# Two graph layers on one core: a new order of the written-out steps, with map, messages and the output product ahead of the four cosines

## The chip, the core and the metric

The kernel runs on one core of a Trainium2 chip. The metric is device time in microseconds (us) from start to end of one execution. The engines of the core are TensorE (PE in the profile; its weight loads are PEld), VectorE (DVE), ScalarE (ACT), GpSimd (POOL) and SyncE (SP, which issues nearly all DMAs). Each works through its own queue in order and waits where an instruction needs what another engine has not finished.

## What is computed

There are 64 graphs of 256 nodes with 512 features, each with an adjacency mask. Two layers follow one another. Cut to what matters:

```python
h = relu(layernorm(x))                      # layer 0, 8 heads of 64
m = h @ map_w.T + map_b
cos_adj = (cosine(m, m) > 0.1) & mask       # per head
p = softmax(where(mask, q(m) @ k(m).T / 8, NEG)) * keep
adj = cos_adj * p
x = x + relu((adj @ (h @ gcn_map_w.T + b)) @ gcn_W.T / (adj.sum(-1) + 1))
h = relu(layernorm(x))                      # layer 1, 4 heads of 64
x = x + softmax(where(mask, q @ k.T / 8, -inf)) @ v @ Wo + bo
```

All products are in float32.

## The kernel before

The graphs are taken one after the other, in a software pipeline over five of them. In round i the kernel works on graph i (its attention and cosines of layer 0), on i+1 (its map, messages, queries and keys), on i+2 (its first layernorm and the transposing of it), on i-1 (layer 1 up to its values) and on i-2 (the output product of layer 1 and the store). The work of a round is cut into 240 small steps with names of two to four letters (`steps_of`, L697 on). The list `ORDER` (L679) gives the order in which they are written out for rounds 2 to 61. `HEAD` and `TAIL` (L1010 on) give it for the opening, with rounds 0 and 1, and for the closing, with rounds 62, 63 and what follows. The whole runs under `tc.manual_schedule()`: the order of the list is the order of each engine's queue. Nothing is moved at run time.

Steps that matter here, with their lines:

- `sc0` to `sc3`: scores of graph i for two heads each, two PSUM banks a step (L475). `ex` takes their exponential (ACT, L482), `mk` multiplies by the mask (DVE, L491), `hv` adds the two halves (POOL, L495).
- `co0` to `co3`: cosines, likewise two banks a step (L512). `un` makes the unit vectors first (DVE, L460). `up` and `fo` read the cosines from PSUM (ACT L521; DVE L528, four instructions a step). `ft` transposes by DMA (SP, L533), `fb` applies that (DVE, L543), `fa` and `fz` add up (POOL, L538).
- Seven products: the matrices are multiplied in halves with seven block products instead of eight (class `Seven`, L303). The steps of one are `X1 Xa X2 Xd X3 Xb X4 Xc X5 Xe X6 Xf X7 Xg`. `1` to `7` are products on PE (L318, L323). `1`, `3`, `4` fill bank u, `2`, `5`, `6`, `7` fill bank z and go on adding to it. `a`, `b`, `c` copy parts of u away, `d`, `e`, `f` add such a copy to z and store a quarter of the result, `g` stores the last. So `5` needs `d`, `6` needs `e`, `7` needs `f`; bank u is free after `c`, bank z after `g`. X is `m` for the map, `s` for the messages, `q` and `k` for queries and keys, `j` and `v` for layer 1's queries with keys and values, `w` for layer 1's output. The adds are DVE's (L350, with L335 and L339 for the copies of `w` and `s`); the copies and the last store of `m`, `q`, `k` are ACT's (L343), those of `j` and `v` ACT's too (L337).
- Left factors on POOL (L295 to L301): `lw` for w, `lm` for q and k, `lb` for j and v, `lh` for m and s. Product `3` needs the first, `5` the second, `6` the third, `4` the fourth.
- `av0`, `av1`: values of layer 0 (L502). `hs` (ACT), `ht` (DMA), `hj` (ACT, L572) turn them. `rt`, `rc`, `rk`, `ho`, `ha` divide and add them to x. `nb`, `pb`, `xb`, `fl`, `tr`, `jb` are the layernorm of layer 1 and its transposing by DMA; `na`, `pa`, `xa`, `pl`, `ta`, `ja` are the same for graph i+2 in layer 0.
- `sd`, `ey`, `my`, `hy`, `ay`, `zb`, `iy`, `sy`, `dv`: attention of layer 1. `sq`, `pn`, `ln`, `ls`, `li`, `sp`: the lengths for the unit vectors. `bo` adds the bias (POOL). `mt` and `ed` prepare the mask.

All PSUM tiles come from one ring of eight banks (`ring`, `bufs=8`). A tile takes the bank that has been free longest in the order of the steps, and waits for the last reader of the tile before it.

Of the kernel before, what the change touches and what calls it, by code (L numbers as in the profile page):

```python
# [158 lines left out]
def fast_path(ctx, tc, a, w, chk, out):  # L159
# [850 lines left out]
    HEAD = """  # L1010
        o.w0 o.na00 o.na01 o.nr0 o.dn0 o.xn00 o.xn01 o.tp00 o.gb o.fm0 o.fm1 o.tq00 o.tp01 o.tq01 o.ed0 o.lh00
        o.lh01 o.lh03 o.bp o.m1 o.fp1 o.lj o.ma o.fm2 o.m2 o.md o.m3 o.fm3 o.fq0 o.fq1 o.q2 o.lo
        o.m5 o.mb o.fo1 o.lh02 o.m4 o.fp2 o.mc o.fq2 o.me o.fp0 o.fo0 o.m6 o.fq3 o.fk0 o.mf o.sq1
        o.fp3 o.bo o.m7 o.mg o.fo3 o.k1 o.k2 o.fk1 o.lm0 o.fk2 o.fk3 0.na o.lm1 0.pa o.lm3 o.lm2
        o.na10 o.q1 o.na11 o.fo2 o.sq0 o.q3 o.k3 o.pn o.qa o.qb o.kb o.qd o.ln o.fs0 o.fs1 o.s1
        o.nr1 o.ka 0.xa0 0.pl00 o.q4 o.qc o.kd o.sa o.fs2 o.q5 o.k4 o.k5 o.s2 o.dn1 o.fs3 o.qe
        o.ex o.lv o.kc o.ke o.xn10 o.xn11 o.ls o.sd o.k6 o.q6 o.kf o.mt0 o.qf o.s3 0.sc2 0.ex2
        0.sc3 o.s5 o.tp10 o.fw0 o.fv0 o.fw1 o.sb o.s4 o.fj0 o.fj1 o.tp11 o.k7 0.mk2 o.li o.sc o.se
        0.hv2 o.s6 o.q7 0.xa1 0.pl10 0.ex3 o.fw2 o.kg o.qg o.tq10 o.tq11 o.sf o.s7 0.sc0 0.sc1 0.mk3
        o.sp o.ed1 0.mt o.fv1 0.un 0.hv3 o.lh10 o.sg 0.ex0 0.co2 0.fo2 0.ex1 0.co1 0.co0 0.co3 0.up2  # L1020
        0.up0 0.ft0 0.m1 0.m3 0.mk1 o.lh12 0.up3 0.ma o.fj2 0.mk0 0.up1 0.fo3 o.lh11 o.lh13 0.hv1 0.s1
        0.s3 0.m2 0.sa 0.mb 0.s2 o.lb o.l3 0.ft2 0.ta00 0.md 0.sb 0.sd 0.m4 0.m5 0.fo1 0.fa3
        0.hv0 0.fa2 0.fa1 0.ed 0.s4 0.ft3 0.mc 0.me 0.m6 0.mf 0.s5 0.m7 0.q1 0.sc 0.fo0 0.k1
        0.se 0.pl01 0.ta01 0.fb3 0.ka 0.sq1 0.qa 0.pl11 0.mg o.fv2 o.fv3 0.ft1 0.k2 0.ta10 0.fb1 0.s6
        0.q2 0.sf 0.s7 0.fa0 0.fz1 0.fz3 0.lm0 0.ta11 0.lm1 0.sq0 0.fb2 0.fb0 0.av0 1.na 0.lm3 0.av1
        0.fz0 0.hs01 0.ja0 0.ja1 0.pn 0.hs00 0.ln 0.kd o.fj3 0.q3 0.qd 0.k3 0.k5 0.kb 0.ht01 0.hs10
        0.hs11 1.m1 0.qb 0.k4 0.ls 0.ht00 0.ht10 0.ht11 0.kc 0.lh0 0.q4 0.qc 0.fz2 0.sm 0.hj00 0.ke
        0.q5 0.to 0.lm2 0.lh2 0.li 0.qe 0.k6 0.q6 0.rt 1.s1 1.s2 1.ma 0.kf 0.qf 0.lh1 1.pa
        0.lh3 0.rc 0.sg 1.rk 0.hj01 0.sp 0.hj10 0.hj11 1.m3 0.k7 0.kg 0.q7 0.qg 1.s3 1.sc2 1.sc1
        1.m2 1.mb 1.ho0 1.ho1 1.ha0 1.ha1 1.nb 1.sa 1.pb 1.ex2 1.xb0 1.sb 1.ex1 1.mk2 1.sd 1.xb1  # L1030
        1.s4 1.m4 1.s5 1.mc 1.un 1.sc0 1.ex0 1.fl00 1.sc3 1.fl01 1.fl10 1.sc 1.se 1.md 1.tr00 1.ex3
        1.co1 1.mk1 1.co0 1.s6 1.tr01 1.fl11 1.mk0 1.tr10 1.up1 1.up0 1.xa0 1.tr11 1.jb0 1.mt 1.sf 1.m5
        1.hv1 1.fo1 1.s7 1.hv0 1.fa1 1.co2 1.jb1 1.hv2 1.sg 1.xa1 1.me 1.fo0 1.fo2 1.fa0 1.lb0 1.lb1
        1.up2 1.ft0 1.pl01 1.ta01 1.co3 1.k2 1.m6 1.j1 1.ja 1.j2 1.mf 1.k1 1.up3 1.pl00 1.mk3 1.hv3
        1.pl10 1.fo3 1.j3 1.v1 1.v3 1.jd 1.m7 1.jb 1.mg 1.lb3 1.j4 1.vb 1.v2 1.v4 1.vc 1.fa2
        1.fa3 1.lb2 1.fb0 1.ka 1.ft1 1.ft2 1.ta00 1.ft3 1.fb2 1.j5 1.fb1 1.kd 1.va 1.jc 1.je 1.lm0
        1.vd 1.fb3 1.av0 1.av1 1.j6 1.q1 1.hs11 1.v5 1.hs00 1.pl11 1.jf 1.ta10 1.ja0 1.fz2 1.fz0 1.j7
        1.ve 1.v6 1.hs01 1.lm1 1.hs10 1.fz3 1.bo1 1.k3 1.jg 1.sd1 1.sd0 1.kb 1.ey1 1.ey0 1.vf 1.my1
        1.q3 1.ta11 1.ht10 1.v7 1.lm3 1.k4 1.sq1 1.qb 1.k5 1.q4 1.kc 1.sq0 1.pn 1.my0 1.ln 1.ke
        1.q2 1.bo0 1.vg 1.ht11 1.ja1 1.ht00 1.hy1 1.hy0 1.fz1 1.lh0 1.ls 1.lm2 1.lh1 1.ht01 1.zb 1.iy  # L1040
        1.sy 1.qa 1.qd o.fw3 1.hj00 1.lh3 1.li 1.sp 1.sm 1.ay 1.to 1.ed 1.lh2 1.q5 1.rt 1.k6
        1.qc 1.qe 1.oy 1.q6 1.hj01 1.kf 1.rc 1.qf 1.k7 1.rq 1.hj10 1.hj11 1.q7 1.qg 1.kg 1.zq
    """.split()
    TAIL = """
        2.rk 2.m1 2.ma 2.sc0 2.ex0 2.sc1 2.sc2 2.ex1 2.ho0 2.ho1 2.ha0 2.dv 2.sc3 2.s1 2.s3 2.w2
        2.s2 2.ex3 2.ha1 2.nb 2.mk3 2.lw0 2.m2 2.pb 2.xb0 2.un 2.sa 2.m3 2.xb1 2.ex2 2.w1 2.lw1
        2.fl00 2.mb 2.sd 2.md 2.sb 2.wa 2.wd 2.mk2 2.fl11 2.s5 2.fl01 2.m4 2.mc 2.mk0 2.m5 2.fl10
        2.s4 2.lw3 2.hv0 2.co0 2.sc 2.me 2.se 2.co2 2.up2 2.up0 2.m6 2.s6 2.w3 2.mk1 2.mf 2.m7
        2.wb 2.fo0 2.mt 2.tr00 2.tr01 2.tr10 2.tr11 2.w4 2.jb0 2.hv2 2.wc 2.hv3 2.w5 2.mg 2.co3 2.lw2
        2.hv1 2.we 2.ft0 2.jb1 2.lb0 2.lb1 2.lm0 2.fo2 2.fo3 2.co1 2.fo1 2.j1 2.lb2 2.lb3 2.fa1 2.rr  # L1050
        2.w6 2.fa0 2.fa3 2.fa2 2.v1 2.up3 2.v3 2.up1 2.lm1 2.j3 2.ja 2.ft2 2.j2 2.wf 2.va 2.w7
        2.v2 2.jd 2.vd 2.jb 2.j4 2.sf 2.v5 2.jc 2.j5 2.q1 2.vb 2.v4 2.ft3 2.je 2.qa 2.vc
        2.wg 2.ft1 2.ve 2.j6 2.k1 2.ka 2.v6 2.jf 2.fb0 2.fz0 2.j7 2.fb1 2.fz1 2.vf 2.lm3 2.v7
        2.sq1 2.jg 2.vg 2.sq0 2.av0 2.fb3 2.hs00 2.hs01 2.pn 2.fz3 2.sd0 2.ey0 2.ht00 2.fb2 2.sd1 2.av1
        2.k2 2.q3 2.ln 2.rq 2.my0 2.ey1 2.fz2 2.hy0 2.my1 2.hy1 2.q2 2.sm 2.zb 2.hj00 2.hs10 2.hs11
        2.ls 2.ht01 2.ht10 2.ht11 2.qb 2.to 2.hj01 2.q4 2.qc 2.rt 2.qd 2.iy 2.kd 2.rc 2.q5 2.hj10
        2.qe 2.hj11 2.k3 2.kb 1.rk 2.lm2 2.q6 2.ay 1.ho0 2.k4 2.kc 2.st 2.k5 2.oy 1.ho1 1.ha0
        1.ha1 2.qf 1.nb 2.li 1.pb 2.ke 2.q7 2.k6 2.kf 2.s7 2.qg 1.xb0 1.fl00 1.xb1 2.k7 2.kg
        2.zq 1.sc0 2.sp 1.un 1.fl01 1.sc1 1.sc2 2.sg 1.fl10 1.sc3 1.ex0 1.co0 1.ex1 2.sy 1.ex2 1.mk0
        1.mk1 1.co2 1.fl11 1.tr00 1.tr01 1.tr10 1.ex3 1.co1 1.rq 1.up0 1.up1 1.up2 1.jb0 1.mk2 c.se0 c.se1  # L1060
        1.mk3 c.se2 c.se3 1.dv 1.fo2 1.lw0 1.co3 1.fo0 1.tr11 1.ft1 1.w1 1.lw1 1.lw3 1.jb1 1.up3 1.w3
        1.fo1 2.bo0 1.rr 1.wa 2.bo1 1.lb0 1.lb1 1.lb3 1.lw2 1.w2 1.wd 1.j2 1.lb2 1.j1 1.w5 1.ja
        1.wb 1.w4 1.ft2 1.ft0 1.ft3 1.fb2 1.fb1 1.v1 1.wc 1.fb0 1.fo3 1.fb3 1.j3 1.av0 1.av1 c.sm0
        c.sm1 1.bo1 c.sm3 c.vs1 c.vs0 1.jb 1.va c.fi c.sm2 1.we 1.w6 c.to c.hb1 1.rt c.hb0 1.wf
        1.rc c.rk 1.w7 1.j4 1.jd 1.j5 1.jc c.hm0 c.hm1 1.je 1.v2 1.vd 1.v3 1.vb 1.j6 1.v4
        1.vc c.hp0 c.nb0 c.hp1 1.jf 1.v5 1.bo0 1.j7 c.nb1 1.jg 1.ve 1.v6 c.nr c.dn c.xn0 c.xn1
        1.vf 1.sd0 1.sd1 1.v7 c.tp0 c.tp1 1.ey0 1.my0 1.ey1 c.rq 1.vg c.tq0 1.my1 1.ay c.tq1 1.hy0
        1.hy1 0.lb0 0.lb1 0.j1 0.ja 1.zb 0.v1 0.lb3 0.j3 1.zq 0.jb 1.iy 0.lb2 0.j2 1.sy 0.j4
        0.jd 0.jc 0.j5 0.v3 0.vb 0.v2 0.je 0.j6 0.va 0.v4 1.oy 0.vd 0.v5 0.jf 0.vc 0.j7
        0.jg 0.ve 0.v6 0.sd0 0.sd1 0.vf 0.v7 0.ey0 0.ey1 0.dv 0.lw0 0.w2 1.wg 0.my0 0.my1 1.st  # L1070
        0.w1 0.lw1 0.w3 0.wa 0.wd 0.wb 0.vg c.zl c.zi0 0.lw3 0.ay c.zm0 0.bo0 0.w5 0.w4 c.zi1
# [336 lines left out]
```

## Time and profile before

| | |
|---|---|
| median of 3 runs | 3538.68 us (3538.03 to 3538.77) |
| the profiled execution | 3538.69 us |
| its span, first to last instruction | 3536.9 us |
| mean granted TensorE clock | 0.999 |
| matmuls | 29365 |
| DMA | 258.30 MB, mean 73 GB/s |
| one round in the middle | 54.67 us |

In a timeline line the columns are start in us, length in us, engine, line of the kernel, operation, what is written and read, shapes (stationary tile, moving tile), and the number of instructions that are merged into the line. In square brackets stands the idle time before it and what ended it. Matmuls overlap, so the length of such a line is a little more than the time to the next start; the starts give the pace. A PE share of 100% only says that some matmul was always under way. A matmul that started late, or ended late, hides a wait in it. Lines of groups end in busy time, mean length in ns, and idle time before the group with what ended most of it. In the list of waits come total us, times and the longest.

### The profile page before, as it was taken

To read this page: it belongs to the slowest core of one execution; us is meant where nothing else is said; L and a number is where in the kernel's file an instruction comes from. 1 tells how busy PE (TensorE), PEld (TensorE's weight loads), DVE (VectorE), ACT (ScalarE), POOL (GpSimd) and SP (SyncE) were. 2 spreads that over 40 slices of the span, in tenths; PEclk is the share of its full clock that TensorE was granted. 3 is DMA by queue.
4 is the path that set the end of the run, shared out by engine and by line. 5 is a ranking of instruction groups with operands and counts; after the bars stand their busy time and mean duration, and the time that the engine had idled before them with its cause. 6 is when DMAs were issued, how large, how long until landed. Compare 5 with 4: busy or idle time off the path is not lost.

```text
span 3536.9 us, 78933 instructions
## 1 busy us (share of the span) xinstructions
PE 3521.0 (100%) x29365; PEld 3090.5 (87%) x29365; DVE 2407.6 (68%) x5037; ACT 2261.2 (64%) x5302; POOL 2693.9 (76%) x2866
## 2 busy tenths in 40 slices
...
DMA packets 650589, 258.30 MB, mean 73 GB/s; under 512 B 561980, under 2 KB 616792, under 8 KB 650200
## 3 DMA queue, kind: packets, MB, share of 16 engines
q1 hardware_dynamic: 649464, 252.62, 32.5%
...
## 4 chain that ended last, share of the span: by engine, by line
PE 98%; DVE 0%; issue 0%; ACT 0%; ACTq 0%; DVEq 0%
PE av L502 10%; PE p_q_z L323 7%; PE p_m_z L323 7%; PE p_s_z L318 7%; PE sc L475 7%; PE p_qk_z L323 6%; PE p_k_z L323 6%; PE co L512 6%; PE p_qk_u L323 5%; PE p_q_u L323 5%; PE p_k_u L323 5%; PE p_m_u L323 5%; PE p_s_u L318 5%; PE sd L475 3%; PE p_o_z L318 3%; PE p_v_z L318 3%
## 5 line engine op out<-in xcount | busy, mean ns | idle before, releaser
L495 POOL TENSOR_TENSOR d<-e 128x512 f32<-128x512 f32 x378 | 532.5, 1422 | 316.2 <-DVE e L491 165.3
L538 POOL TENSOR_TENSOR d<-d,e 128x512 f32<-128x512 f32 x504 | 633.4, 1273 | 68.4 <-DVE e L543 65.2
L489 DVE SCALAR_TENSOR_TENSOR e<-mask,e 128x1024 f32<-128x1024 bf16 x128 | 214.4, 1677 | 245.4 <-ACT e L482 245.3
L260 POOL COPY flat<-xn 128x512 uint16<-128x512 uint16 x252 | 310.7, 1261 | 58.4 <-ACT xn L252 57.5
L491 DVE TENSOR_TENSOR e<-e,mask 128x1024 f32<-128x1024 f32 x256 | 328.4, 1324 | 4.3 <-ACT e L482 2.8
L528 DVE SCALAR_TENSOR_TENSOR e<-co,e 128x256 f32<-128x256 f32 (+1 forms) x1024 | 293.9, 349 | 52.6 <-ACT up L521 33.1
L482 ACT ACTIVATE e<-sc 128x512 f32<-128x512 f32 x512 | 270.8, 601 | 75.3 <-PE sc L475 75.2
L521 ACT ACTIVATE up<-co,below 128x128 bf16<-128x128 f32 x512 | 166.8, 371 | 195.7 <-PE co L512 121.4
L252 ACT ACTIVATE xn<-xs,shift,rs 128x512 f32<-128x512 f32 x250 | 196.9, 811 | 74.8 <-POOL shift L242 74.8
L475 PE MATMUL sc<-qT,kT 64*128 64x256 f32 x2048 | 239.0, 383 | 0.0
L502 PE MATMUL av<-e,sem 128*64 128x256 f32 x2048 | 235.5, 382 | 0.0
L512 PEld LDWEIGHTS co<-nT 64*128 64x128 f32 x2048 | 185.0, 186 | 53.9 <-issue 34.6
L512 PE MATMUL co<-nT 64*128 64x128 f32 (+1 forms) x2048 | 228.9, 338 | 0.5 <-DVE nT L460 0.5
L475 PEld LDWEIGHTS sc<-qT,kT 64*128 64x128 f32 x2048 | 192.0, 186 | 29.3 <-DVE wo L83 0.3
L502 PEld LDWEIGHTS av<-e,sem 128*64 128x64 f32 x2048 | 141.2, 137 | 85.7 <-issue 20.2
L295 POOL TENSOR_TENSOR own<-own 128x128 f32<-128x128 f32 x63 | 52.0, 825 | 181.0 <-DVE own L674 181.0
L572 ACT COPY sem<-heads 128x512 uint16<-128x512 uint16 x252 | 187.0, 780 | 1.6 <-DMA heads<-avs 1.6
L443 POOL TENSOR_TENSOR lengths<-lengths,root 128x16 f32<-128x16 f32 x64 | 185.8, 2903 | 1.6 <-DMA lengths<-rn 1.6
L482 ACT ACTIVATE e<-sd 128x512 f32<-128x512 f32 x256 | 138.7, 599 | 66.4 <-PE sd L475 66.4
L205 DVE BATCH_NORM_STATS2 st<-xs 128x6 f32<-128x512 f32 x256 | 172.6, 674 | 5.8 <-DMA xs<-in_x_dram 3.6
L276 ACT COPY h1T<-turn 128x1024 uint16<-128x1024 uint16 x126 | 169.7, 1348 | 7.2 <-DMA turn<-flat 7.1
L272 ACT COPY hT<-turn 128x1024 uint16<-128x1024 uint16 x124 | 171.2, 1382 | 0.0
...
## 6 DMA issues: line engine op xcount, KB each, us to landing
...
nT<-by_rn SPq DMA_DIRECT2D x128, 256.0 KB
...
far<-up SPq DMA_TRANSPOSE x256
heads<-avs SPq DMA_TRANSPOSE x252
```

Source lines behind the costliest of these rows:

```text
L260: copy(getattr(g, what)[:, t, k, :], g.xn[t].bitcast(U16).rearrange("p (d k) -> p k d", k=2)[:, k, :])
L318: nc.tensor.matmul(region, src[:, c, :], self.wt[:, block, c, :], start=p not in self.opened, stop=True, skip_group_check=True)
L323: nc.tensor.matmul(region[:, f, :], self.wt[:, block, c, f * P:(f + 1) * P], src[:, c, :], start=p not in self.opened, stop=True, skip_gro ...
L475: nc.tensor.matmul(ps[s][:, j, :], rows[h, c, j * P:(j + 1) * P], cols[h, c, :], start=True, stop=True)
L482: nc.scalar.activation(e[:, s, :], p.rearrange("p j q -> p (j q)"), AF.Exp, scale=SCALE)
L489: nc.vector.scalar_tensor_tensor(e, m, 0.5, e, op0=ALU.is_lt, op1=ALU.mult)
L491: nc.vector.tensor_mul(e, e, m)
L495: nc.gpsimd.tensor_add(d, e[:, :, :S], e[:, :, S:])
L502: nc.tensor.matmul(av[s * DH:(s + 1) * DH, n, :], vs[:, j, (h0 + s) * DH:(h0 + s + 1) * DH], q[:, s, j * S:(j + 1) * S], start=(j == 0), s ...
L512: nc.tensor.matmul(ps[s][:, j, j * P:], g.nT[h, c, j * P:(j + 1) * P], g.nT[h, c, j * P:], start=(j == 0), stop=True, skip_group_check=True)
L528: nc.vector.scalar_tensor_tensor(e, p.rearrange("p j q -> p (j q)")[:, lo:hi], THRESHOLD, e, op0=ALU.is_gt, op1=ALU.mult)
L538: nc.gpsimd.tensor_add(g.d[c][:, :, q], g.d[c][:, :, q], g.e[c][:, :, lo:hi])
```

## The change

The three lists are written in a new order. Each holds the same steps as before (240, 512 and 451), so no instruction is added, removed or altered; the queues of the engines and the choice of banks change with the order. In `ORDER` the old list starts with the four scores and spreads map, messages and output product from before the cosines to after them (`m6`, `s6`, `m7`, `s7` come after `co1`). The new one starts with `s1 s3 m1 m3`, and has all products of `s`, `m` and `w` ahead of `co0`; queries and values follow the cosines.

```diff
     ORDER = """
-        rk sc2 ho1 ho0 sc1 sc3 ha0 dv ha1 ex2 sc0 ex3 lw0 lw1 nb w2
-        w1 w3 s1 m1 s3 wa wd wb lw3 w4 mk3 mk2 ex1 mt w5 lw2
-        s2 m3 wc we sa sd pb w6 xb0 xb1 ma fl01 s5 wf w7 m2
-        un fl00 tr00 hv3 fl10 fl11 wg md sb mb m4 tr01 ex0 st m5 tr10
-        mk1 mk0 hv1 mc s4 sc co3 co0 hv0 tr11 up3 fo3 ld me rq co2
-        jb0 hv2 co1 se fo1 m6 mf s6 sf up1 k1 fo0 fa3 jb1 up2 lb0
-        na lb1 lb3 pa fa1 m7 rr up0 j1 v1 fa0 v3 j2 mg lm0 ft3
-        ja vb va v4 xa0 j3 vc jd lb2 q1 jb pl01 j4 j5 ft2 xa1
-        pl11 pl10 ft0 fo2 fb0 fz0 v2 vd pl00 jc ft1 ta00 je lm1 fa2 lm3
-        s7 v5 j6 ve v6 jf vf fb2 fb3 qa fb1 fz1 q3 v7 vg ta01
-        j7 k3 fz2 jg sd0 sd1 sq0 ey0 my0 sq1 av0 ey1 ta10 av1 fz3 hs00
-        hs01 qb my1 ay hy0 hy1 bo1 pn ta11 ht01 ht00 ln sm zb ls hs10
-        kb ja0 lm2 hs11 ht11 ka ja1 lh0 ed q2 q4 k2 iy k4 kd k5
-        qc hj00 kc ht10 sy lh1 bo0 to hj01 hj10 qd q5 ke qe k6 rt
-        q6 kf li rc k7 lh2 oy sg qf sp lh3 zq q7 hj11 kg qg
+        s1 rk s3 ho0 ho1 ha0 ha1 nb sa m1 m3 sc0 ex0 sc3 ex3 sb
+        mb pb mt xb0 fl00 sc2 sc1 s2 s4 xb1 ex1 dv mk0 mk3 sd lw0
+        fl01 tr00 tr01 lw1 fl10 lw3 m2 hv0 ma un s5 sc se w1 w3 mk1
+        s6 sf m4 ex2 mc md w2 m5 wa wb wd lw2 fl11 hv1 me w4
+        w5 wc we m6 mf w6 wf s7 w7 m7 co0 co3 wg tr10 mk2 co2
+        tr11 jb0 mg up0 sg fo0 jb1 co1 st fo1 hv3 q1 fo3 up1 up2 v2
+        ld up3 lm0 ft3 bo0 hv2 v1 lb2 va fo2 vd lb0 lb1 j2 fa0 lb3
+        ft1 j1 j3 v3 k1 jb rq ja jd ka vb lm1 j4 q2 v5 ft0
+        v4 j5 vc jc qa na fa2 pa fa3 ve rr xa0 pl01 ft2 pl00 fb0
+        lm3 fz0 fa1 qd k3 k2 v6 je j6 vf kd jf fb2 q3 j7 xa1
+        v7 pl10 pl11 qb q4 fb3 jg vg sq0 qc sd0 fb1 sd1 av0 fz3 fz1
+        ey0 ey1 hs01 my0 av1 ta01 ta00 ta11 ta10 ja0 fz2 my1 ay hs00 sq1 kb
+        ht01 pn sm hy1 ja1 hy0 ed zb k4 ln ht00 lm2 q5 lh0 lh1 lh3
+        ls hs10 ht10 hs11 hj00 ht11 kc iy qe lh2 k5 li hj01 to zq hj10
+        oy bo1 sy ke q6 k6 rt qf kf sp hj11 q7 k7 kg rc qg
     """.split()
```

`HEAD` and `TAIL` are reordered in the same manner. Of them, the end of the closing and the place of `c.wu` (nine matmuls on the unit matrix, 18 instructions) are spoken of below:

```diff
     TAIL = """
...
-        c.zm1 0.wc 0.bo1 c.po0 0.we 0.lw2 0.w6 0.wf c.po1 c.oa0 0.w7 c.wu c.oa1 c.st0 0.wg c.st1
-        0.st c.zk 0.rr
...
+        1.zb c.hm0 1.zq 1.v6 1.vf 1.iy c.hp0 c.hp1 c.nb0 c.nb1 c.nr 1.v7 1.vg 1.ay c.wu c.dn
+        c.xn0 c.xn1 1.oy 0.bo1 c.tp0 1.sy 0.dv c.tp1 c.tq0 c.tq1 0.lb0 0.j2 0.j1 0.j3 0.v2 0.v1
...
+        0.we 0.ay c.zi0 c.zm0 c.zi1 0.w6 c.zm1 c.zk c.po0 0.wf 0.w7 0.wg c.oa0 0.st c.st0 0.rr
+        c.po1 c.oa1 c.st1
     """.split()
```

More of the change, by code (lines that the diff above doesn't have):

```diff
@@ L1010, in fast_path @@
     HEAD = """
[L1011 to L1039, printed above, removed]
@@ L1040, in fast_path @@
-        1.q2 1.bo0 1.vg 1.ht11 1.ja1 1.ht00 1.hy1 1.hy0 1.fz1 1.lh0 1.ls 1.lm2 1.lh1 1.ht01 1.zb 1.iy
-        1.sy 1.qa 1.qd o.fw3 1.hj00 1.lh3 1.li 1.sp 1.sm 1.ay 1.to 1.ed 1.lh2 1.q5 1.rt 1.k6
-        1.qc 1.qe 1.oy 1.q6 1.hj01 1.kf 1.rc 1.qf 1.k7 1.rq 1.hj10 1.hj11 1.q7 1.qg 1.kg 1.zq
+        o.na00 o.na01 o.nr0 o.dn0 o.w0 o.xn00 o.xn01 o.tp00 o.tq00 o.tp01 o.tq01 o.fm0 o.fm1 o.m2 o.gb o.fm2
+        o.fm3 o.m1 o.ed0 o.lh00 o.lh01 o.lh03 o.lh02 o.m3 o.ma o.md o.fp1 o.fq0 o.mb o.fp3 o.fq1 o.m4
@@ new lines, in fast_path @@
+        o.m5 o.mc o.me o.fq2 o.fq3 o.fp0 o.lv o.m6 o.mf o.sq1 o.bp o.na10 o.q1 o.m7 o.fo0 o.fo3
+        o.bo o.fk0 o.mg o.sq0 o.fp2 o.k1 o.fo2 o.lm2 o.pn o.fk1 o.fo1 o.k2 o.ka 0.na o.lm0 o.s1
+        o.q3 o.k3 o.lm1 o.l3 o.fk2 o.fs0 o.kd o.q2 o.lm3 o.k5 o.kb o.ln o.fs1 o.fs2 o.fk3 o.mt0
+        o.ls o.fs3 o.lj o.fv0 o.qa o.qb o.k4 o.q4 o.qd o.q5 o.kc o.ke o.na11 o.qc o.k6 o.qe
+        o.q6 o.kf o.qf o.nr1 1.na o.li 0.pa o.ed1 o.dn1 1.pa o.k7 o.q7 o.s3 o.xn10 o.sb o.s2
+        o.sp o.ex o.kg o.qg 0.xa0 0.xa1 0.sc1 0.pl00 0.ex1 0.sc2 0.sc0 o.fj0 o.fj1 o.sa o.sd 0.mk1
@@ new lines, in fast_path @@
+        o.xn11 0.ta00 o.s4 0.ex2 o.s5 o.sc o.se 0.sc3 o.s6 0.un 0.hv1 o.sf o.tp11 o.tp10 0.ex0 0.mk0
+        0.ex3 0.mk3 o.tq10 o.s7 o.tq11 0.co1 0.up1 o.sg o.lh10 0.co3 0.hv0 0.pl01 0.fo1 0.fa1 0.co2 0.co0
+        0.up0 0.ta01 0.ft0 0.fo0 o.lh11 0.up3 0.pl10 0.m1 0.m3 0.hv3 0.s2 0.ma 0.s1 0.up2 0.m2 0.fo3
+        0.md 0.mb 0.s3 0.mk2 0.fa0 0.fb0 o.lh13 0.fa3 o.lh12 0.q2 0.pl11 0.m4 0.m5 0.mc 0.hv2 0.ft1
+        0.fb1 0.ft3 0.me 0.ft2 0.sb 0.fz0 0.mt 0.av0 0.m6 0.fz1 0.sa 0.sd 0.s4 0.mf 0.m7 1.xa0
```

71 lines of the change are left out of this document (44 added, 27 removed).

## The prediction, on record before the changed kernel was run

> **What bounds the kernel now.** I read the page first (shares, then the chain that ended last), then TensorE's timeline over two rounds in the middle, then the busy time of the cosines' stretch by windows, then VectorE's timeline of the same stretch and the list of waits.
>
> ```profile
> span 3536.9 us, 78933 instructions
> PE 3521.0 (100%) x29365; PEld 3090.5 (87%) x29365; DVE 2407.6 (68%) x5037; ACT 2261.2 (64%) x5302; POOL 2693.9 (76%) x2866
> PE 98%; DVE 0%; issue 0%; ACT 0%; ACTq 0%; DVEq 0%
> ```
>
> TensorE is the chain: 98% of it. A busy share of 100% leaves nothing to gain only if every matmul runs at its own pace. The starts in the timeline test that:
>
> ```profile
> 1499.52 3.72 PE L475 MATMUL sc<-qT,kT 64*128 64x256 f32 x31
> ...
> 1509.81 0.60 PE L318 MATMUL p_o_z<-wo,own 128*128 128x256 f32 x2
> 1510.44 1.13 PE L318 MATMUL p_s_z<-wc,sh_hT 128*128 128x256 f32 x4
> 1511.41 0.59 PE L318 MATMUL p_o_z<-wo,own 128*128 128x256 f32 x2
> 1511.84 1.05 PE L323 MATMUL p_m_z<-hT,wm 128*128 128x128 f32 x8
> 1512.73 1.06 PE L323 MATMUL p_m_u<-sh_hT,wm 128*128 128x128 f32 x8
> ...
> 1515.48 3.61 PE L512 MATMUL co<-nT 64*128 64x256 f32 x32
> 1519.02 1.16 PE L323 MATMUL p_m_z<-sh_hT,wm 128*128 128x128 f32 x8
> ...
> 1554.18 3.72 PE L475 MATMUL sc<-qT,kT 64*128 64x256 f32 x32
> ```
>
> One graph is one round of 54.67 us (1499.52 to 1554.18). From start to start, eight 128x128 matmuls take 0.89 us (1511.84 to 1512.73) and two of 128x256 0.43 us (1511.41 to 1511.84). Against that pace two places are long. The two p_o_z (w6) at 1509.81 take 0.63 instead of 0.43, and the four p_s_z (s5) after them 0.97 instead of 0.87: together 0.3 us. And the four cosines:
>
> ```profile
> 1515.48:1516.23 0.75, 0.75 (x8) 0.71 (x10) 0.00 (x0) 0.00 (x0) 1.00 0.41 94
> 1516.24:1516.88 0.64, 0.64 (x12) 0.59 (x10) 0.00 (x0) 0.45 (x2) 1.00 1.39 138
> 1516.89:1517.54 0.65, 0.65 (x12) 0.58 (x8) 0.64 (x3) 0.17 (x1) 1.00 0.09 11
> 1517.55:1519.02 1.47, 1.47 (x12) 0.99 (x8) 0.53 (x3) 0.00 (x0) 1.00 0.66 206
> ```
>
> Windows of the tile co (columns: length, then busy PE, PEld, DVE, ACT, clock, DMA). A cosine costs 0.65 us, the fourth 1.47. A change of array shape costs 0.1 at the end, so 0.72 us of the fourth is waiting, counted as busy. Who is late:
>
> ```profile
> 1509.96 0.42 DVE L350 TENSOR_TENSOR sem<-p_s_z,u2p_s 128x256 f32<-128x256 f32 x1
> ...
> 1516.90 1.15 DVE L528 SCALAR_TENSOR_TENSOR e<-co,e 128x256 f32<-128x256 f32 x4 [0.55 <-ACT up L521]
> PEld p_s_z L318 <- DVE sem L350: 26.5, 60, 0.4
> ```
>
> The first is sd, which ends at 1510.38; s5 starts 0.06 later. It stands in DVE's queue behind two masks (L491, 2.76 us) and wc, we and sa. The second is fo3. It reads the first cosine's two banks, and these are the banks that the fourth takes: in the step list map and messages still hold two of eight (p_m_z, p_s_z), three cosines take the other six. fo3 ends at 1518.05, and the second half of the fourth starts some 0.15 us later. The granted clock is 1.00 throughout.
>
> So a round has 0.30 + 0.72 + some 0.05 (small gaps in p_k_z, p_v_u, p_n) = 1.07 us that isn't matmul pace. The six changes of shape into and out of sc, co, sd, av, pn, zb cost another 1.5 us, which both orders pay: TensorE's list has the same blocks in both.
>
> **The change, part by part.** No instruction is added or removed; every list is a permutation. I walk the new round on TensorE's own axis, T = 0 at s1, with the paces above (s 0.87, m/q/k/j 0.89, w 0.43, v 0.45, sc 0.865, co 0.655, 0.1 on each side of a change of shape): sc0 3.6, s2 7.3, s5 10.0, w1 10.9, s6 11.7, m5 13.9, m6 15.7, w6 16.6, m7 18.3, the cosines 19.3 to 22.0, q1 22.1, j2 24.0, j4 28.0, j6 33.8, sd0 37.9, av0 39.8, pn 45.2, end 53.6. So 53.6 us is the floor of a round.
>
> *Banks.* A new bank is the one that has been free longest in step order. In the new list the cosines take those of sc, ex2 (2), mc, wc, wg, mg and sg: none of another cosine. The latest are mg (ACT) and sg (DVE). m7's last matmul ends at 19.4; mg is 0.62 behind it, 20.0. wg is done at 18.9, mk2 (1.22) at 20.1, sg at 20.5. co1 starts at 21.4. The 0.72 goes; its cover is 0.9 us of slack. After the block q1 needs fo0's first half (21.2, due 22.1), v1 and j2 fo1's two (22.9 and 23.5, due 23.6 and 24.0), j1 fo3's (24.1, due 24.9). The wait isn't passed on, but j2 has only 0.3 us over a weight load.
> *s5.* In the new list m2 stands ahead of it. DVE does rk, ho, ha, nb until T = 3.9, sa, sb, dv until 5.5, mk0 and mk3 (ex0 ends at 5.9) until 8.3, sd 8.8. Due 10.0. The 0.30 goes.
> *Steps one product apart.* s5-s6, m5-m6, w5-w6 stand 0.87 apart: 0.2 for the matmul to land, 0.42 for DVE, so 0.24 is over. The old list has the same spacing (v2, s7, v5) at no cost, so I take nought; the upper end is 0.1 us each.
> *sc.* sc1 takes the banks of ex0. sc0 is read from 4.8 on, the second half ends at 5.9; due 6.3. Nothing.
> *POOL, now a queue with lw, hv and fl mixed.* The lw are due 11.3 to 16.6, and come at 10.5 to 15.2 (fl00 starts at 8.1, when xb0 ends). From lm0 (after mg, 20.05) lm0, bo0, hv2, lb2, lb0, lb1, fa0, lb3 are 0.73 + 1.27 + 1.28 + 3x0.75 + 1.27 + 0.73 = 7.5: lb3 at 27.5, due 28.0 at j4. Nothing, with 0.3 to spare.
> *ACT.* jb0 now stands ahead of mg. It waits for the transposes tr00 and tr10, whose rows are 1.2 us of issue each; tr10 follows fl10 (13.1), so jb0 can run from 17 to 18.3. Nothing. sq1 ends at 44.8 behind ja0, pn is due 45.2: nothing, barely.
> *SP.* Transposes (1.2 us each) and the four small moves are the same; li now goes ahead of sy. li's rows (2.9 us on POOL) end at T = -0.9, sy lands near 3, dv is at 4.8. sp lands near 4, un runs at 8.8. Nothing.
>
> *A rule that speaks against this.* The Trainium skill, "SBUF — State Buffer", section "Who interferes with whom", says that a VectorE instruction with two SBUF inputs and a GpSimd instruction that reads SBUF exclude each other for the whole instruction. The trace agrees:
>
> ```profile
> L495 POOL TENSOR_TENSOR d<-e 128x512 f32<-128x512 f32 x378 | 532.5, 1422 | 316.2 <-DVE e L491 165.3
> L260 POOL COPY flat<-xn 128x512 uint16<-128x512 uint16 x252 | 310.7, 1261 | 58.4 <-ACT xn L252 57.5
> ```
>
> The copy takes 606 ns at best and 1617 at most, the sum 1259 and 2296. With the mean rows the walk above has no stall, 53.6. With full exclusion at the two places where the new queues meet with least slack: mk1 starts behind fl10 (up to 0.6 late), so sf and md are late for m5 by 0.2, and 0.1 of weight load is then uncovered; fb0 stands behind fa3 (until 32.5), so je ends at 33.6 and j6 (33.8) loses up to 0.25. That is 0.55 a round, 54.15. Nothing would be gained below the floor. I take 0.1 a round, near the rows' means, because POOL alone has 3.9 us idle ahead of lm0 that absorbs such delays, and keep 0 and 0.55.
>
> *A second rule.* "Perfetto Trace Analysis", "Identifying the Most-Contended Engine", judges TensorE by its weight loads: here 87%, so 13% or 446 us open. The spacing says 1.07 of 54.67 us, 2%. I use the spacing: much of the 13% is shapes whose loads are shorter than their matmuls.
>
> *Opening and closing.* Waits of this kind in the old opening: 0.51 and 0.60 us idle at 46.1 and 53.4, about 2 us with uncovered loads. The old closing ends with w7 and 2.0 us of warm matmuls ahead of the last check; the new one puts these ahead of c.tp0, with only 3 us of products between hb0 and there against 8 before. Taken together -1 us, from -4 to +4.
>
> Sum: 3538.7 (the profiled run's 3538.69; its span is 3536.9, and the median of the runs 3538.68) - 60x1.07 = -64.2, + 60x0.1 = +6, - 1: **3479 us**.
>
> **Rivals.** (a) Forecast, 3470 to 3491: the loop runs nearly at TensorE's pace. Chance 0.67. (b) The lock comes back at m5 and j6, 0.55 a round: 3538.7 - 64 + 33 - 1 = 3507. For it: the L495 mean 1422 over a best of 1259; against: idle time on POOL. 0.19. (c) The cosine wait only moves to v1, j2 or j1, because DVE needs 4x1.15 us for four fo and the banks are wanted one by one: 0.72 returns, 3479 + 43 = 3522. Against: the slacks above. 0.06. (d) Slower: DVE's closing chain (hj11, rk, ho, ha, nb) now stands directly ahead of sa, sb, dv, mk0, mk3, sd, and s5 waits for that. Its slack is 0.45 at mk0 and 1.0 at s5, together 1.5 us. If the head transposes land so that it is over 2.7 us late, the loss passes 1.2 us a round and the kernel is slower; at 3.0 late it is 1.6 a round, 3474 + 96 = 3570. Against: ht11 should be issued 4 us before hj11 is due. 0.06. That nothing is changed (within 0.2%, about what a measurement can tell from none) needs new waits of just 1.07: 0.02.
>
> The range 3470 to 3508 leaves out (c), (d) and half of (b)'s upper part. Faster by over 0.2%: a, b, c, 0.92; the same 0.02; slower 0.06.
>
> **What would show it.** A round of 53.6 to 53.8 us; four equal cosines of 0.65; no wait of p_s_z for sem (26.5 us before); POOL's lb3 ending before j4. I am wrong if p_m_z, p_qk_z or p_s_u show starts that are longer than their pace by 0.1 or more in each round.

## The result, and the profile after

The changed kernel takes 3479.8 us (median of 4 runs, 3479.2 to 3481.6) against 3538.4 (3537.8 to 3538.8) for the kernel before on the same chip: a ratio of 0.9835, 95% interval 0.9818 to 0.9852. The profiled execution took 3480.2 us. First its span, the busy shares, and the shares of the chain that ended last:

```profile
span 3478.2 us, 79003 instructions
PE 3465.0 (100%) x29365; PEld 3080.5 (89%) x29365; DVE 2353.8 (68%) x5037; ACT 2240.9 (64%) x5302; POOL 2590.1 (74%) x2866
PE 98%; DVE 1%; DMA 1%; issue 0%; ACT 0%; DVEq 0%; ACTq 0%
```

These shares say nothing of the gain: PE is busy 100% of the span and 98% of the chain, as before. PE's busy time fell by 56 us with the same 29365 matmuls, because matmuls that started late are now on time. The two places, in TensorE's timeline of a round (T = 0 at 1634.40):

```profile
1643.50 1.05 PE L323 MATMUL p_m_z<-hT,wm 128*128 128x128 f32 x8
1644.39 1.03 PE L318 MATMUL p_s_z<-wc,sh_hT 128*128 128x256 f32 x4
1645.25 1.03 PE L318 MATMUL p_o_u<-wo,own 128*128 128x256 f32 x4
...
1653.72 2.89 PE L512 MATMUL co<-nT 64*128 64x256 f32 x32
1656.54 1.16 PE L323 MATMUL p_q_u<-mT,wq 128*128 128x128 f32 x8
```

s5, the p_s_z at 1644.39, starts 0.89 after m2 and takes 0.86, its own pace. All 32 cosine matmuls take 2.82 us from start to start; they took 3.54. The four by themselves, in the windows of the tile co:

```profile
1653.70:1654.46 0.76, 0.74 (x8) 0.70 (x10) 0.00 (x0) 0.00 (x0) 1.00 0.17 67
1654.47:1655.11 0.64, 0.64 (x12) 0.59 (x10) 0.00 (x0) 0.44 (x2) 1.00 1.01 394
1655.12:1655.77 0.65, 0.65 (x12) 0.60 (x10) 0.63 (x3) 0.18 (x1) 1.00 0.86 331
1655.78:1656.53 0.75, 0.75 (x12) 0.59 (x8) 0.51 (x2) 0.00 (x0) 1.00 0.00 0
```

The fourth takes 0.75 instead of 1.47: 0.65 and the change of shape. VectorE's timeline has what the two wait for:

```profile
1640.42 2.36 DVE L491 TENSOR_TENSOR e<-e,mask 128x1024 f32<-128x1024 f32 x2
1642.84 0.42 DVE L350 TENSOR_TENSOR sem<-p_s_z,u2p_s 128x256 f32<-128x256 f32 x1
...
1654.41 0.42 DVE L339 TENSOR_TENSOR sem<-p_s_z,bc 128x256 f32<-128x256 f32 x1
1655.14 1.15 DVE L528 SCALAR_TENSOR_TENSOR e<-co,e 128x256 f32<-128x256 f32 x4 [0.31 <-ACT up L521]
```

sd (1642.84) ends 1.1 us before s5 starts. sg (1654.41) gives its bank back at 1654.83, before the fourth cosine's start at 1655.78; fo0 ends only at 1656.29, which nobody waits for now. Where the time went, with the matmuls of the opening, of the 60 rounds and of the closing counted off in order:

| us | opening | 60 rounds | closing | a usual round |
|---|---|---|---|---|
| before | 132.79 | 3280.25 | 123.87 | 54.67 |
| after | 131.33 | 3221.17 | 125.69 | 53.65 |
| difference | -1.46 | -59.08 | +1.82 | -1.02 |

Two more lines changed that were not on the path. GpSimd's copy, and its sum of two halves, got shorter:

```profile
L495 POOL TENSOR_TENSOR d<-e 128x512 f32<-128x512 f32 x378 | 478.8, 1281 | 196.3 <-DVE e L489 188.7
L260 POOL COPY flat<-xn 128x512 uint16<-128x512 uint16 x252 | 160.5, 639 | 124.6 <-ACT xn L252 124.6
```

The copy fell from 1261 to 639 ns, the sum from 1422 to 1281: they collide less with VectorE. So three explanations stood after the result. My theory: two separate waits of TensorE, for the banks of the fourth cosine (0.72 a round) and of s5 for sd (0.30). First rival: fewer collisions of VectorE and GpSimd. Second rival: the new opening and closing carry part of it.

### The profile page after: what moved, and what is told of

It reads as the page before. It is cut to its first block, busy times and chain, and to the rows that moved or that the text cites. A ratio compares the mean times of both kernels' runs of the same rounds, so it can differ in the third digit from the quotient of the medians.

```text
span 3478.2 us, 79003 instructions
## 1 busy us (share of the span) xinstructions
PE 3465.0 (100%) x29365; PEld 3080.5 (89%) x29365; DVE 2353.8 (68%) x5037; ACT 2240.9 (64%) x5302; POOL 2590.1 (74%) x2866
## 4 chain that ended last, share of the span: by engine, by line
PE 98%; DVE 1%; DMA 1%; issue 0%; ACT 0%; DVEq 0%; ACTq 0%
PE av L502 10%; PE sc L475 7%; PE p_s_z L318 7%; PE p_qk_z L323 7%; PE p_q_z L323 7%; PE p_k_z L323 6%; PE p_m_z L323 6%; PE co L512 5%; PE p_k_u L323 5%; PE p_q_u L323 5%; PE p_qk_u L323 5%; PE p_m_u L323 5%; PE p_s_u L318 5%; PE sd L475 4%; PE p_v_z L318 3%; PE p_o_z L318 3%
## 5 line engine op out<-in xcount | busy, mean ns | idle before, releaser
L495 POOL TENSOR_TENSOR d<-e 128x512 f32<-128x512 f32 x378 | 478.8, 1281 | 196.3 <-DVE e L489 188.7
L491 DVE TENSOR_TENSOR e<-e,mask 128x1024 f32<-128x1024 f32 x256 | 326.1, 1295 | 3.7 <-ACT e L482 3.3
L489 DVE SCALAR_TENSOR_TENSOR e<-mask,e 128x1024 f32<-128x1024 bf16 x128 | 154.6, 1230 | 246.0 <-ACT e L482 246.0
L528 DVE SCALAR_TENSOR_TENSOR e<-co,e 128x256 f32<-128x256 f32 (+1 forms) x1024 | 283.3, 349 | 48.3 <-PE co L512 26.4
L260 POOL COPY flat<-xn 128x512 uint16<-128x512 uint16 x252 | 160.5, 639 | 124.6 <-ACT xn L252 124.6
L238 POOL TENSOR_SCALAR shift<-mv 128x2 f32<-128x2 f32 x125 | 27.8, 222 | 283.3 <-DVE mv L206 283.3
L521 ACT ACTIVATE up<-co,below 128x128 bf16<-128x128 f32 x512 | 154.8, 367 | 78.2 <-DVE e L528 60.5
L572 ACT COPY sem<-heads 128x512 uint16<-128x512 uint16 x252 | 199.2, 793 | 7.4 <-DMA heads<-avs 6.9
L276 ACT COPY h1T<-turn 128x1024 uint16<-128x1024 uint16 x126 | 170.9, 1358 | 35.2 <-DMA turn<-flat 35.2
L512 PE MATMUL co<-nT 64*128 64x256 f32 (+1 forms) x2048 | 185.8, 330 | 0.0
L512 PEld LDWEIGHTS co<-nT 64*128 64x128 f32 x2048 | 162.2, 187 | 20.0 <-issue 1.1
```

The lines of the kernel that those rows point to most:

```text
L491: nc.vector.tensor_mul(e, e, m)
L495: nc.gpsimd.tensor_add(d, e[:, :, :S], e[:, :, S:])
L512: nc.tensor.matmul(ps[s][:, j, j * P:], g.nT[h, c, j * P:(j + 1) * P], g.nT[h, c, j * P:], start=(j == 0), stop=True, skip_group_check=True)
L528: nc.vector.scalar_tensor_tensor(e, p.rearrange("p j q -> p (j q)")[:, lo:hi], THRESHOLD, e, op0=ALU.is_gt, op1=ALU.mult)
L572: nc.scalar.copy(bits[:, k, c], g.heads[:, k, c])
```

## The experiments

**The new order of the rounds alone.** `ORDER` of the changed kernel, `HEAD` and `TAIL` of the kernel before.

> The new ORDER for the 60 rounds, with the opening and the closing of the kernel before. If the gain is made in the rounds (60 x 1.02 measured in the trace of the changed kernel), a round takes 53.65 us and the time is 3538.4 - 59.1 = 3479.3 us, from 3477 to 3482. If the opening and closing lists carry a good part of the gain, it is well above: 3500 or more.

Measured: 3480.2 us (3480.2 to 3480.7), ratio 0.9838 (0.9821 to 0.9854). The usual round is 53.65, the loop 3220.85. The opening and closing lists carry nothing: with the new ones the opening is 1.3 us shorter, the closing 0.75 longer. The second rival falls.

**Only the mask moved.** One word of the old `ORDER`:

```diff
-        w1 w3 s1 m1 s3 wa wd wb lw3 w4 mk3 mk2 ex1 mt w5 lw2
-        s2 m3 wc we sa sd pb w6 xb0 xb1 ma fl01 s5 wf w7 m2
+        w1 w3 s1 m1 s3 wa wd wb lw3 w4 mk3 ex1 mt w5 lw2
+        s2 m3 wc we sa sd mk2 pb w6 xb0 xb1 ma fl01 s5 wf w7 m2
```

> The order of the kernel before with one step moved: the second mask, mk2, goes from ahead of wc, we, sa and sd to just behind sd in VectorE's queue. TensorE's order is untouched. Theory (s5 waits only because sd stands behind the masks): sd ends near 10.1 us of the round, s5 is due at 10.7, the 0.31 us goes, and the four p_s_z take 0.87: 3538.4 - 60 x 0.31 = 3520 us. Rival (the gain of the change comes from TensorE's order or from fewer collisions of VectorE and GpSimd, not from this wait): within 3 us of 3538.

Measured: 3543.6 us (3543.0 to 3544.6), ratio 1.0017 (1.0010 to 1.0024): slower than before, a miss. Its timeline (w6 at 1676.70, s5 at 1677.14, then w7):

```profile
1676.11 0.42 DVE L350 TENSOR_TENSOR sem<-p_s_z,u2p_s 128x256 f32<-128x256 f32 x1
...
1676.45 1.46 DVE L491 TENSOR_TENSOR e<-e,mask 128x1024 f32<-128x1024 f32 x1
...
1676.70 0.60 PE L318 MATMUL p_o_z<-wo,own 128*128 128x256 f32 x2
...
1677.14 1.03 PE L318 MATMUL p_s_z<-wc,sh_hT 128*128 128x256 f32 x4
1677.83 0.41 DVE L350 TENSOR_TENSOR xs<-p_o_z,u5p_o 128x256 f32<-128x256 f32 x1
...
1678.30 0.30 PEld L318 LDWEIGHTS p_o_z<-wo,own 128*128 128x128 f32 x2 [0.53 <-DVE xs L350]
1678.30 0.70 PE L318 MATMUL p_o_z<-wo,own 128*128 128x256 f32 x2
```

sd is on time and s5 starts 0.44 after w6, at once. But wf (1677.83) now stands behind the mask, and w7 starts 1.16 after s5 instead of 0.86. The 0.31 is gone and 0.40 has come in its place, one product later. I had looked at the slack of the step that I freed and not at the next one in the queue.

**s5 behind m2, on TensorE.** So the same wait was taken away on the other side, in the old `ORDER`, as the change does it:

```diff
-        s2 m3 wc we sa sd pb w6 xb0 xb1 ma fl01 s5 wf w7 m2
+        s2 m3 wc we sa sd pb w6 xb0 xb1 ma fl01 m2 wf w7 s5
```

> The order of the kernel before with two products moved on TensorE: m2 goes between w6 and w7, and s5, which stood there, behind w7. VectorE's queue keeps its order, and each step still has a product of 0.9 us between it and the one that it waits for. Theory (0.31 us a round is s5's wait for sd; with mk2 moved away the wait only went on to w7): s5 is due 1.3 us later, after sd, w7 still after wf: 3538 - 18 = 3520 us, from 3516 to 3524. Rival (VectorE's queue is so full here that whichever product comes next waits): 3535 us or more.

Measured: 3519.7 us (3519.2 to 3520.1), ratio 0.9948 (0.9933 to 0.9964); round 54.36, 0.31 below 54.67. The timeline, w6, m2, w7, s5 and m4, has each start at its pace (0.43, 0.89, 0.44, 0.86):

```profile
1665.00 0.60 PE L318 MATMUL p_o_z<-wo,own 128*128 128x256 f32 x2
1665.43 1.05 PE L323 MATMUL p_m_z<-hT,wm 128*128 128x128 f32 x8
1666.32 0.60 PE L318 MATMUL p_o_z<-wo,own 128*128 128x256 f32 x2
1666.76 1.03 PE L318 MATMUL p_s_z<-wc,sh_hT 128*128 128x256 f32 x4
1667.62 1.05 PE L323 MATMUL p_m_u<-sh_hT,wm 128*128 128x128 f32 x8
```

The first wait is shown: 0.31 a round.

**The fourth cosine later, in the old order.** If co1 only waits for fo3's banks, it is enough to start it later.

```diff
-        mk1 mk0 hv1 mc s4 sc co3 co0 hv0 tr11 up3 fo3 ld me rq co2
-        jb0 hv2 co1 se fo1 m6 mf s6 sf up1 k1 fo0 fa3 jb1 up2 lb0
-        na lb1 lb3 pa fa1 m7 rr up0 j1 v1 fa0 v3 j2 mg lm0 ft3
+        mk1 mk0 hv1 mc s4 sc me se co3 co0 hv0 tr11 up3 fo3 ld rq co2
+        jb0 hv2 m6 mf co1 fo1 s6 sf m7 up1 k1 fo0 fa3 jb1 up2 lb0
+        na lb1 lb3 pa fa1 rr up0 j1 v1 fa0 v3 j2 mg lm0 ft3
```

> The order of the kernel before, with the fourth cosine, co1, put behind m6, so that the banks that fo3 gives back are free when it starts; me and se go ahead of the cosines in VectorE's queue, and m7 ahead of k1, so that nothing else waits. The output and all banks stay the same. Theory (the fourth cosine's extra 0.72 us is the wait for fo3's banks): the cosine takes 0.65 plus the two added changes of shape, some 0.39 a round: -0.33 a round, 3538.4 - 20 = 3519 us. Rival (the fourth cosine is slow for another reason: VectorE, or its own operands): it stays at 1.3 us or more, and the changes of shape come on top, 3538 + 23 = 3562 us.

Measured: 3560.3 us (3559.7 to 3561.0), ratio 1.0063 (1.0046 to 1.0080). The time is the rival's, the mechanism is not. The starts from m6 on:

```profile
1691.80 1.16 PE L323 MATMUL p_m_z<-sh_hT,wm 128*128 128x128 f32 x8
1692.89 0.92 PE L512 MATMUL co<-nT 64*128 64x256 f32 x8
1693.74 1.13 PE L318 MATMUL p_s_z<-wc,sh_hT 128*128 128x256 f32 x4
1694.71 1.05 PE L323 MATMUL p_m_z<-hT,wm 128*128 128x128 f32 x8
1695.60 1.06 PE L323 MATMUL p_k_u<-mT,wk 128*128 128x128 f32 x8
1696.76 1.16 PE L323 MATMUL p_qk_u<-h1T,wqk 128*128 128x128 f32 x8
1697.90 0.71 PE L318 MATMUL p_v_u<-wv,h1T 128*128 128x128 f32 x4
```

The cosine takes 0.85 from start to start, that is 0.65 and its changes of shape: its wait is gone. But j1 (p_qk_u) starts 1.16 behind k1 (p_k_u) instead of 0.89, and v1 (p_v_u) 1.14 behind j1; 0.1 of the latter is j1's first weight load, which is no longer covered, and v1 itself takes 0.54 instead of 0.45 for the same reason. The list of waits of this run says what ended them:

```profile
PEld p_qk_u L323 <- ACT h1T L276: 22.4, 60, 0.7
PEld p_v_u L318 <- ACT up L521: 10.3, 60, 0.2
```

The first needs jb1 (L276), which ScalarE does behind up1; up1 reads the cosine that I had delayed. v1 needs a bank that up0 (L521) frees, behind jb1. Again the wait had moved on, this time along ScalarE's queue. In every fourth round j1 starts some 0.35 later still, 5 us in all; why every fourth is not known. So jb1 went ahead of up1:

```diff
-        jb0 hv2 m6 mf co1 fo1 s6 sf m7 up1 k1 fo0 fa3 jb1 up2 lb0
+        jb0 hv2 m6 mf co1 fo1 s6 jb1 sf m7 up1 k1 fo0 fa3 up2 lb0
```

> As the kernel before with the fourth cosine behind m6, and with jb1 put ahead of up1 in ScalarE's queue, since j1 waited for jb1 there (0.36 us) and v1 for up0 behind it (0.25). Theory: with these two gone the 0.72 of the cosine less 0.39 for two more changes of shape is left, -0.33 a round: 3538 - 20 = 3518 us. If the wait only moves along ScalarE's queue, it stays at 3545 to 3560.

Measured: 3518.7 us (3517.8 to 3518.9), ratio 0.9945 (0.9928 to 0.9961); round 54.34, 0.33 below 54.67. The three cosines and the fourth, as windows of the tile co:

```profile
1670.15:1672.32 2.17, 2.16 (x24) 1.91 (x24) 0.71 (x3) 0.62 (x2) 1.00 0.68 108
1673.40:1674.26 0.86, 0.85 (x8) 0.69 (x8) 0.00 (x0) 0.00 (x0) 1.00 1.01 275
```

**Both repairs together.** The two first versions together, mk2 behind sd and the cosine behind m6 without jb1, had been expected at 3500 us if their gains added. They took 3565.3 us (3565.0 to 3566.3), ratio 1.0077 (1.0061 to 1.0094): it is their losses that add, 0.10 and 0.37 a round on average, to 0.46. So the two repairs that hold were put together. The three edits on the old `ORDER`: s5 behind m2, the cosine behind m6, jb1 ahead of up1.

```diff
-        s2 m3 wc we sa sd pb w6 xb0 xb1 ma fl01 s5 wf w7 m2
+        s2 m3 wc we sa sd pb w6 xb0 xb1 ma fl01 m2 wf w7 s5
...
-        mk1 mk0 hv1 mc s4 sc co3 co0 hv0 tr11 up3 fo3 ld me rq co2
-        jb0 hv2 co1 se fo1 m6 mf s6 sf up1 k1 fo0 fa3 jb1 up2 lb0
-        na lb1 lb3 pa fa1 m7 rr up0 j1 v1 fa0 v3 j2 mg lm0 ft3
+        mk1 mk0 hv1 mc s4 sc me se co3 co0 hv0 tr11 up3 fo3 ld rq co2
+        jb0 hv2 m6 mf co1 fo1 s6 jb1 sf m7 up1 k1 fo0 fa3 up2 lb0
+        na lb1 lb3 pa fa1 rr up0 j1 v1 fa0 v3 j2 mg lm0 ft3
```

> Both repairs in the order of the kernel before: s5 behind m2, and the fourth cosine behind m6 with jb1 ahead of up1. Theory (two separate waits): the gains add, 3538 - 18.5 - 19.2 = 3500 us, from 3497 to 3504. The 20 us that then lie between it and the changed kernel are the two added changes of shape, 0.39 x 60 = 23, less small gaps.

Measured: 3500.1 us (3499.6 to 3500.7), ratio 0.9893 (0.9878 to 0.9908); round 54.03, 0.64 below 54.67: the gains of 0.31 and 0.33 add. Two changes of shape were added. In this run's timeline the three cosines and the fourth take 2.17 and 0.85, together 0.20 more than the four in the changed kernel (2.82), and m6 and s6 on the two sides of the fourth take 0.09 and 0.10 more: 0.39. Less that the round is 53.64, the changed kernel's to 0.01. And its groups on GpSimd are those of the kernel before:

```profile
L495 POOL TENSOR_TENSOR d<-e 128x512 f32<-128x512 f32 x378 | 532.4, 1421 | 268.5 <-DVE e L489 148.0 <-DVE e L491 120.5
...
L260 POOL COPY flat<-xn 128x512 uint16<-128x512 uint16 x252 | 310.8, 1260 | 58.4 <-ACT xn L252 58.4
```

Both waits are gone while the copy still takes 1260 ns and the sum 1421. The fewer collisions on GpSimd are a by-product that the time does not show. The first rival falls.

**The banks again, from the other side.** In the changed kernel TensorE's order stays; only the words that give banks back are moved. Once both:

```diff
-        tr11 jb0 mg up0 sg fo0 jb1 co1 st fo1 hv3 q1 fo3 up1 up2 v2
-        ld up3 lm0 ft3 bo0 hv2 v1 lb2 va fo2 vd lb0 lb1 j2 fa0 lb3
+        tr11 jb0 up0 fo0 jb1 co1 mg sg st fo1 hv3 q1 fo3 up1 up2 v2
+        ld up3 ft3 bo0 hv2 v1 lb2 va fo2 vd lb0 lb1 j2 fa0 lb3 lm0
```

> The changed kernel with mg and sg (the two steps that give back the banks of map and messages) written behind co1, and lm0 behind lb3 so that GpSimd's queue doesn't wait for mg. TensorE's order is untouched; co1 must now take both banks of the first cosine. Theory (the fourth cosine waits for what fo reads): fo0's two halves end at 21.36 and 21.89 us of the round, co1 is due at 21.39, and started 0.14 behind in the kernel before: the second half is 0.64 late, with 0.07 as in the kernel before 0.7 a round: 3480 + 60 x 0.7 = 3522 us, from 3515 to 3526. Rival (it is the place of the cosines behind map and messages that counts, not the banks): within 4 us of 3480.

Measured: 3522.7 us (3522.1 to 3523.8), ratio 0.9957 (0.9941 to 0.9974); round 54.38. Once sg alone:

```diff
-        tr11 jb0 mg up0 sg fo0 jb1 co1 st fo1 hv3 q1 fo3 up1 up2 v2
+        tr11 jb0 mg up0 fo0 jb1 co1 sg st fo1 hv3 q1 fo3 up1 up2 v2
```

> The changed kernel with only sg written behind co1: co1 takes mg's bank and the first one that fo0 gives back. Theory: that bank is free at 21.36, the half that takes it starts 0.14 later, at 21.50 instead of 21.39: 0.1 a round, 3480 + 7 = 3487 us, from 3482 to 3492. If the size of the wait does not follow from which half of fo0 is waited for, it is as far off as with both banks, 3515 or more.

Measured: 3492.3 us (3491.2 to 3494.3), ratio 0.9870 (0.9853 to 0.9886); round 53.85. The window of the fourth cosine with both banks late:

```profile
1674.74:1676.21 1.47, 1.47 (x12) 0.99 (x8) 0.53 (x3) 0.00 (x0) 1.00 0.02 7
```

and with one:

```profile
1660.94:1661.88 0.94, 0.94 (x12) 0.80 (x8) 0.53 (x3) 0.00 (x0) 1.00 0.00 0
```

1.47 is the old kernel's number to the digit, in the new order of TensorE: the bank is the cause. With one bank the step is 0.20 a round, not 0.1: the late half starts 0.12 behind, about as said, and its second matmul 0.29 after the first instead of 0.22; the weight load isn't covered then. In the profiled execution another 2 us are in the closing, 127.8 there.

**What a late sd would cost.** sd behind un and mk1 in the changed kernel, which is the prediction's slower case (d), made by hand.

```diff
-        mb pb mt xb0 fl00 sc2 sc1 s2 s4 xb1 ex1 dv mk0 mk3 sd lw0
-        fl01 tr00 tr01 lw1 fl10 lw3 m2 hv0 ma un s5 sc se w1 w3 mk1
+        mb pb mt xb0 fl00 sc2 sc1 s2 s4 xb1 ex1 dv mk0 mk3 lw0
+        fl01 tr00 tr01 lw1 fl10 lw3 m2 hv0 ma un mk1 sd s5 sc se w1 w3
```

> The changed kernel with sd behind un and a third mask, mk1, in VectorE's queue: un 8.3 to 9.5 us of the round, mk1 to 10.7 (10.95 with GpSimd beside it), sd to 11.05 or 11.35. s5 is due at 10.0. Theory: s5 waits for it, 1.1 to 1.4 us and 0.1 of uncovered weight load a round: 3480 + 72 to 90 = 3552 to 3570 us. Rival (such a wait is taken up elsewhere in the round, since other engines are idle for a quarter of it): under 3500 us.

Measured: 3591.3 us (3590.9 to 3591.8), ratio 1.0151 (1.0134 to 1.0168); round 55.49. The wait is 1.84 a round, above the range. The timeline of VectorE, GpSimd and TensorE (un is L460, mk1 L491, sd L350, s5 the p_s_z):

```profile
1694.50 0.68 POOL L260 COPY flat<-xn 128x512 uint16<-128x512 uint16 x1 [2.02 <-ACT xn L252]
...
1694.63 1.63 DVE L460 TENSOR_TENSOR nT<-nT,mT 128x1024 f32<-128x1024 f32 x1
...
1695.15 1.42 POOL L295 TENSOR_TENSOR own<-own 128x128 f32<-128x128 f32 x1
...
1696.21 1.45 DVE L491 TENSOR_TENSOR e<-e,mask 128x1024 f32<-128x1024 f32 x1
...
1697.58 0.41 DVE L350 TENSOR_TENSOR sem<-p_s_z,u2p_s 128x256 f32<-128x256 f32 x1
...
1698.04 0.73 PEld L318 LDWEIGHTS p_s_z<-wc,sh_hT 128*128 128x128 f32 x4 [1.76 <-DVE sem L350]
```

un has started 0.13 after the copy and ends 1.08 after the copy's end. The left factor that starts beside un lasts 1.42 instead of 0.45 and ends 0.31 after un does; mk1 then ends 1.09 after the left factor's end. The two engines take turns. My range had one collision in it, the queue had two. So the collisions do cost time where the longer instruction stands ahead of a step that TensorE waits for.

**A version that might beat both.** The changed kernel with the `TAIL` of the kernel before, and sq1 next to sq0:

```diff
-        v7 pl10 pl11 qb q4 fb3 jg vg sq0 qc sd0 fb1 sd1 av0 fz3 fz1
-        ey0 ey1 hs01 my0 av1 ta01 ta00 ta11 ta10 ja0 fz2 my1 ay hs00 sq1 kb
+        v7 pl10 pl11 qb q4 fb3 jg vg sq0 sq1 qc sd0 fb1 sd1 av0 fz3 fz1
+        ey0 ey1 hs01 my0 av1 ta01 ta00 ta11 ta10 ja0 fz2 my1 ay hs00 kb
```

> A version that might beat both: the changed kernel with the closing list of the kernel before, and with sq1 next to sq0 in ScalarE's queue (in four rounds of the changed kernel pn waits for sq1, 0.9 us in all). The closing should cost 124.9 us as in the run with the new order alone, instead of 125.7: 3480 - 0.8 - 0.9 = 3478.3 us, from 3477 to 3480. If the closing list makes no difference, 3479 to 3480.

Measured: 3478.4 us (3478.2 to 3479.5, 5 runs), ratio 0.9833 (0.9819 to 0.9846). The closing takes 124.96 instead of 125.69, and the three rounds that were over 0.1 us longer because pn waited for sq1 are gone; one other round is now 0.2 longer, ahead of zb. Against the changed kernel's 0.9835 the interval doesn't separate the two.

## Why the prediction was right

3479 was forecast, 3479.8 measured; case (a). The mechanism was right: two waits of TensorE, each with the cause named. That the sum is right to 1 us is in part luck: the 6 us set aside for the lock of VectorE and GpSimd were not needed for it, and other small losses of 5.3 us, named below, took their place. By its steps:

- *The 1.07 of stall.* Right in size and cause: 0.31 (s5) and 0.72 (cosine) are shown each by itself. Of the third term, 0.05 of small gaps, 0.03 goes (p_k_z and p_v_u); the 0.02 in p_n is still there. So the spacing, with 1.07 a round, had read rightly what there was to gain, and not the 13% in which no weights were loaded: PEld's share rose only to 89%.
- *The floor of 53.6.* The usual round is 53.65; the 0.05 above the floor is w6's, below.
- *Banks.* mg ends at T = 20.0 and sg at 20.4, forecast 20.0 and 20.5; co1 starts at 21.4. The wait was not passed on: q1, v1, j2 and j1 start at their pace. That this needed checking is shown by the two repairs that failed: there it was passed on.
- *s5.* nb ended at 4.8 where I had 3.9, yet sd at 8.85 where I had 8.8: the slack of case (d) was there, 1.1 us.
- *Steps one product apart.* Taken at nought, with 0.1 as upper end. Of the three, w5-w6 costs 0.05 a round, 3.2 us in all, the others nothing. w6 is the p_o_z at 1650.95, we the add that it needs:

```profile
1650.36 0.42 DVE L350 TENSOR_TENSOR xs<-p_o_z,u3p_o 128x256 f32<-128x256 f32 x1
...
1650.95 0.65 PE L318 MATMUL p_o_z<-wo,own 128*128 128x256 f32 x2
1651.44 1.03 PE L318 MATMUL p_s_z<-wc,hT 128*128 128x256 f32 x4
```

  we ends at 1650.78. w6's weights are loaded only after that, and its second matmul comes 0.27 after the first instead of 0.22, so w6 takes 0.49 to the next start instead of 0.43. The forecast had 0.24 to spare at such a step, but counted to the matmul's start; w5's weight load starts 0.21 ahead of its matmul.
- *POOL.* lb3 ended at 27.4, forecast 27.5; j4, which needs it, starts at 28.1.
- *The lock.* I kept 0.1 a round, and it cost nothing that shows: the residue of 0.05 is the term above. It occurred, though. mk1 took 1.51 instead of 1.22 and md ended at 13.57, as in case (b), but m5 was due at 13.9; je ended at 33.3, before j6. GpSimd's idle time ahead of lm0 was 2.3 us where I had 3.9. The Trainium skill's rule ("SBUF — State Buffer", "Who interferes with whom") is borne out by the run with the late sd; what it costs is decided by the slack behind it. In the old kernel it may have had a part in the first wait: mk2 took 1.63 there, and with 1.22 sd would have been in time. That is worked out, not run.
- *Opening and closing.* Forecast -1, measured -1.46 + 1.82 = +0.4. In the opening the gain came, if less than the 2 us of waits that I had counted. For the closing the forecast has no number of its own, and the loss there, 1.82, is more than its sum allows for. With the old closing list behind the new rounds (the first experiment) it takes 124.94, so the new list accounts for 0.75 of the 1.82. The nine products on the unit matrix (warm) now stand ahead of p_t, and cost nothing there:

```profile
3442.94 2.27 PE L1008 MATMUL warm<-ident 128*128 128x128 f32 x18
3444.62 1.00 DVE L223 TENSOR_SCALAR xn<-xs,mv,rs 128x512 f32<-128x512 f32 x2 [0.82 <-POOL rs L218]
3445.31 1.09 PE L230 MATMUL p_t<-ident,xn 128*128 128x128 f32 x8
```

  p_t reads xn, whose first half is written only at 3445.17; p_t's first weight load starts 0.11 later. TensorE would have waited there without the nine products. Which waits make up the 1.82 is not shown.

- *Not foreseen.* Some rounds are longer than the rest, by 1.9 us in all. In three pn waits for sq1, "nothing, barely" in the walk: ScalarE's second exponential of layer 1 is over 1 us late there. In three more (42, 51, 53, counted from 0) TensorE loses 0.3 each at different products; these come back at the same rounds in other runs of the new order, though not in all, and why is open. In the old order one round, 54, is 0.3 longer. Together the longer rounds cost 1.6 us more than before.

The terms sum to -59.2 in the forecast and -58.7 in the trace: -59.1 in the rounds (forecast -58.2), +0.4 in the opening and closing (forecast -1). In the rounds the forecast had +6 for the lock; the trace has 3.2 for w6, 1.6 for the longer rounds, and 0.5 by which the stalls that went are less than the 64.2.
